# One maximum instruction for two heads, steps in the scores' ring, and loads one per chunk, in a two-layer attention kernel

## The chip, the core and the metric

The kernel runs on one core of a Trainium2 chip. The metric is the device time of one execution in microseconds, the median of several runs. The engines are TensorE (PE in the profile, its weight loads PEld), VectorE (DVE), ScalarE (ACT), GpSimd (POOL) and SyncE (SP), which here issues nearly all DMAs.

## What is computed

Two transformer layers over x (4 batches, 512 rows, 320 columns), all in float32, with a context of 1601 rows of 192 for each batch. A layer is self-attention, cross-attention over the context and a gated feed-forward, each with its own norm and residual:

```python
h1 = _ln(x, n1_g, n1_b)
x = _attn(h1, h1, q1, k1, v1, o1_w, o1_b, heads) + x
h2 = _ln(x, n2_g, n2_b)
x = _attn(h2, context, q2, k2, v2, o2_w, o2_b, heads) + x
h3 = _ln(x, n3_g, n3_b)
a, g = jnp.split(h3 @ ff_w1 + ff_b1, 2, axis=-1)
ff = a * jax.nn.gelu(g, approximate=False) @ ff_w2 + ff_b2
return ff + x
```

`_attn` is the usual softmax attention with 20 heads of 16 columns. The feed-forward's inner width is 1280.

## The kernel before

**Units.** The work is a list of units in order. In each layer there are 20 self-attention units (4 batches by 5 groups of 4 heads), 20 cross-attention units and 4 feed-forward units. The four heads of a group lie in four slots of 32 partitions, so that matmuls with 32 rows of contraction can run in the four row groups of TensorE side by side.

**Chunks and maxima.** An attention unit goes over its keys in chunks of 128: 4 chunks for self, 13 for cross. In `main` a chunk has two halves. Each half computes the transposed scores of two heads (`score`, tile st, line 1004), followed by the exponentials on ScalarE (line 1010, tile pr). Beside them it runs two matmuls for the *next* unit: those of `full_one` (tile sps, line 844) make the scores again with queries on the partitions, and VectorE takes their row maxima (line 852). The maxima, negated, become an extra row of the next unit's queries (`max_reduce`, `max_end`; DMAs q<-turned), so that the exponentials need no further subtraction. The rest of 65 keys in the cross-attention is done by `rest_two` (lines 858 and 868). After the two halves come the value products of the chunk before (`values`, tile av, line 1024, copied to vo by ScalarE and added to o by GpSimd at line 1041), then steps, then possibly extra rounds of four maxima, when `give` finds that the next units are owed more than the halves can hold.

**Steps.** Everything else is a step in one of several chains: queries (line 648, evacuated at 660), keys (674, 686), keys of the context (704, 714), values (779, 786 and 797, 806), projection of the attention's output (952, added to x at 959), norms and their transposes (461, 468), and the context's transposes (545). `steps` picks the one that is due first while a credit lasts; a round counter (two rounds to a chunk) stands for time. [...]

**Banks.** The eight PSUM banks are two rings of four: ps_st for scores and value products, ps_m for the maxima's scores and, in the main loop, the steps (`step_bank`). `quarter_banks` takes two of each in turn. In the feed-forward (`ff_main`) the values part of the gate is in ps_st and the gate part in ps_m. The last attention unit before a feed-forward has no maxima to make and spreads its four scores over both rings.

**Loads.** Inputs are loaded through SP's queue. `loads` is a queue of functions; one is run in each unit, after the maxima of the next unit have been finished (`c == u.nch - 3`). One such function issues all DMAs of a stage: `load_cross` 19, `load_self` 15, `load_out` 3. `load_first` (the feed-forward's first weights) is issued at once before the last cross-attention unit. The two functions rows_of_ones (line 132 and 135, GpSimd) are entries of this queue too. In layer 0 `add_context` turns the context by blocks and saves it to DRAM with one DMA; in layer 1 it is loaded back with one DMA and a wait of 8 rounds.

Of the kernel before, what the change touches and what calls it, by code (L numbers as in the profile page):

```python
# [19 lines left out]
FF = 4 * D  # L20
# [45 lines left out]
def kernel(ctx: ExitStack, tc: tile.TileContext, x, context, ws, out):  # L66
# [29 lines left out]
    ps_m = ctx.enter_context(tc.tile_pool(name="ps_m", bufs=4, space=PSUM))  # L96
# [53 lines left out]
    def load_x(b):  # L150
        src = x[b].rearrange("(c p) d -> p c d", p=P)
        for t in range(NQ) if b == 0 else (slice(NQ),):
            dma(out=xs[b][:, t], in_=src[:, t])
        loaded[b] = clock["round"]
# [23 lines left out]

    def load_rows(t, w, chunks):
        for k, at, n in chunks:  # L180
            dma(out=t[:n, k, :], in_=w[at : at + n, :])
# [22 lines left out]
    def load_self(l):  # L204
        load_norm(l, 0)
        load_rows(wq1, ws[l]["q1"], DK)
        load_rows(wk1, ws[l]["k1"], DK)
        load_rows(wv1, ws[l]["v1"], DK)

    def load_out(l, name):  # L210
        load_rows(wo, ws[l][name], DK)

    def load_cross(l):
        load_norm(l, 1)
        load_rows(wq2, ws[l]["q2"], DK)
        load_rows(wv2, ws[l]["v2"], CK)
        for t, n in ((wk_q, "k2"), (wv_q, "v2")):
            for i in range(4):
                dma(out=t[i * 32 : (i + 1) * 32], in_=ws[l][n].rearrange("(k p) d -> p k d", p=32))

    def load_ff(l):
        def small():
            load_norm(l, 2)
            with nc.allow_non_contiguous_dma(reason="a vector's elements go to partitions"):
                dma(out=b1, in_=ws[l]["ff_b1"].rearrange("(c p) -> p c", p=P))
            for half in range(2):
                dma(
                    out=w1r[half * REST : (half + 1) * REST, :],
                    in_=ws[l]["ff_w1"][2 * P :, half * FF : (half + 1) * FF],
                )  # L230

        loads.append(small)
        second = ws[l]["ff_w2"].rearrange("(c p) f -> p c f", p=P)
        for c in (slice(0, NHC // 2), slice(NHC // 2, NHC)):
            loads.append(lambda c=c: dma(out=w2[:, c], in_=second[:, c]))


    def load_first(l):

        load_rows(w1, ws[l]["ff_w1"], FK)  # L240
# [57 lines left out]

    chains = {n: deque() for n in ("divide", "project", "slots", "norm", "context", "early", "proj", "values")}
# [6 lines left out]

    start = {"on": True, "both": False, "quad": False}

    def step_bank(shape, name):

        if start["on"] and not start["both"]:
            return ps_st.tile(shape, F32, tag="st", name=name)
        return ps_m.tile(shape, F32, tag="m", name=name)
# [206 lines left out]
    def add_context(l, b, put, due, free):  # L520
        s = {}

        def tiles():
            s["cT"] = one.tile([P, KB, QT + 32], F32, tag="ctxT", name="ctxT")
            s["tail"] = one.tile([CK[0][2], 2, TAIL], F32, tag="tail", name="tail")

        def load():
            tiles()
            dma(out=s["cT"], in_=saved[b])
            dma(out=s["tail"], in_=saved_tail[b])  # L530
            s["round"] = clock["round"]

        if l:
            add("context", 0.0, load, due - 14, free)
            add("context", 0.0, lambda: put(s), due - 2, yes, lambda: clock["round"] >= s["round"] + 8)
            return

        def turn(i):
            if i == 0:
                tiles()  # L540
            c0, n = CGRP[i]
            t, _ = ctx_in.pop((b, i))
            for c in range(n):
                at = (c0 + c) * 32
                nc.vector.transpose(s["cT"][:, :, at : at + 32], t[:, c, :])
            if i + 2 < len(CGRP):
                load_context(b, i + 2)
            if i + 1 == len(CGRP):
                dma(out=saved[b], in_=s["cT"])
                s["last"] = t  # L550

        def tail():
            ps = step_bank([P, 2, P], "cps")
            for k, at, w in CK:
                nc.tensor.transpose(ps[:w, k, :TAIL], s["last"][:TAIL, 0, at : at + w], ident[:TAIL, :TAIL])
            w = CK[0][2]
            nc.scalar.copy(s["tail"], ps[:w, :, :TAIL])
            dma(out=saved_tail[b], in_=s["tail"])
            put(s)

        for i in range(len(CGRP)):
            add(
                "context", LIGHT, lambda i=i: turn(i), due - 2 * (len(CGRP) - i), free if i == 0 else yes,
                lambda i=i: clock["round"] >= ctx_in[b, i][1] + 4,
            )
        add("context", 0.3, tail, due)

# [30 lines left out]
    def add_proj(u):  # L598
# [97 lines left out]
        def keys_of_context():  # L696

            pss = quarter_banks("kps")
# [13 lines left out]
            for a, ps in enumerate(pss):  # L712
                copy = nc.vector.tensor_copy if a % 2 else nc.scalar.copy
                copy(stage[:, a, :], ps[:, : HALF + 32])
# [43 lines left out]
    def quarter_banks(name):  # L758

        return [  # L760
            pool.tile([P, 512], F32, tag=tag, name=name) for pool, tag in ((ps_st, "st"), (ps_m, "m")) * 2
        ]

    def add_values(u):
# [24 lines left out]
        def values_of_context(i, s):  # L789
# [3 lines left out]
            pss = quarter_banks("vps")  # L793
# [10 lines left out]
            for a, ps in enumerate(pss):  # L804
                copy = nc.vector.tensor_copy if a % 2 else nc.scalar.copy
                copy(vals[:, 4 * s + a, h0:h1, 0:DH], ps[:, :w].rearrange("p (h d) -> p h d", d=DH))
# [22 lines left out]
    def max_pairs(u):  # L829
# [7 lines left out]
        def max_bank(j):  # L837
            if start["both"] and j % 2 or start["quad"] and j == 1:
                return ps_st.tile([P, 512], F32, tag="st", name="sps")
            return ps_m.tile([P, 512], F32, tag="m", name="sps")  # L840

        def full_one(t, s, j):
            ps = max_bank(j)
            nc.tensor.matmul(  # L844
                ps,
                lhsT=u.q[j * SLOT : (j + 1) * SLOT, t * P : (t + 1) * P],
                rhs=u.kT[j * SLOT : (j + 1) * SLOT, u.k0 + s * 512 : u.k0 + (s + 1) * 512],
                start=True,
                stop=True,
            )  # L850
            to = u.nm[:, j * NQ + t : j * NQ + t + 1] if ns == 1 else u.pm[:, t, j, s : s + 1]
            return lambda: nc.vector.tensor_reduce(to, ps, AX.X, ALU.max, negate=(ns == 1))  # L852

        def rest_two(heads):
            pss = [max_bank(j) for j in heads]
# [10 lines left out]
            def reduce():  # L866
                for j, ps in zip(heads, pss):
                    nc.vector.tensor_reduce(
                        u.pm[:, :, j, full],
                        ps[:, : NQ * rest].rearrange("p (t w) -> p t w", w=rest),  # L870
# [7 lines left out]
            deque(  # L878
                [lambda t=t, s=s, j=j: full_one(t, s, j) for j in heads] for s in range(full) for t in range(NQ)
            )  # L880
# [115 lines left out]
    def main(u, give, nxt):  # L996
# [3 lines left out]
        def score(c, j, pool=ps_st, tag="st"):  # L1000
            r = min(P, u.nkeys - c * P)
            rows = slice(j * SLOT, (j + 1) * SLOT)
            st = pool.tile([P, N], F32, tag=tag, name="st")
# [41 lines left out]
        for c in range(u.nch):  # L1045
            extra = []
            if last:

                round_of(
                    [  # L1050
                        lambda j=j, ring=ring: score(c, j, *ring)
                        for j, ring in zip(range(HG), ((ps_st, "st"), (ps_m, "m")) * 2)
                    ],
                    [],
                )
# [13 lines left out]
            start["quad"] = True  # L1069
# [4 lines left out]
            start["quad"] = False  # L1074
            if not last and c == u.nch - 3:
                max_reduce(nxt)
                max_end(nxt)
                if loads:
                    loads.popleft()()
# [21 lines left out]
    def ff_main(u, give, nxt):  # L1101
# [20 lines left out]
        rings = ((ps_st, "st"), (ps_m, "m"))  # L1122

        def full(c, i):
            ps = rings[i][0].tile([P, 512], F32, tag=rings[i][1], name="fps")
# [22 lines left out]
        for c in range(0, NHC, 2):  # L1148

            beside(True, 2)  # L1150
            pss = [[full(c, 0), full(c, 1)]]
            beside(False, 2)
            pss.append([full(c + 1, 0), full(c + 1, 1)])
# [24 lines left out]
    def before(u):  # L1178
# [6 lines left out]
        if u.kind == "cross" and u.m == B * G - 1:  # L1185
            load_first(u.l)
# [4 lines left out]
    def after(u):  # L1191

        stage[u.b] += 1
        if u.b == B - 1:
            load_bias(u.l, ("self", "cross", "ff").index(u.kind) + 2)
            if u.kind == "self":
                loads.append(lambda: load_out(u.l, "o2_w"))
            if u.kind == "cross" and u.l + 1 < L:
                loads.append(lambda: load_out(u.l + 1, "o1_w"))
            if u.l + 1 < L:  # L1200
                if u.kind == "ff":
                    for k in kbuf[1:]:
                        rows_of_ones(k, False)
                    loads.append(lambda: load_cross(u.l + 1))
                    load_ff(u.l + 1)
                elif u.kind == "self":
                    loads.append(lambda: load_self(u.l + 1))
# [63 lines left out]
    load_x(0)  # L1271
    load_self(0)
# [22 lines left out]
    load_x(1)  # L1295
    rows_of_ones(kbuf[0][:, 4 * QT :])
    for k in kbuf[1:]:
        loads.append(lambda k=k: rows_of_ones(k))
    loads.insert(0, lambda: load_x(2))
    loads.append(lambda: load_out(0, "o1_w"))  # L1300
    loads.append(lambda: load_x(3))
    loads.append(lambda: load_cross(0))
    load_ff(0)
# [7 lines left out]
    for i, u in enumerate(units):  # L1311
        nxt = units[i + 1] if i + 1 < len(units) else None
        before(u)
        if u.kind == "ff":

            flush()
            until(lambda: u.hT is not None, "norm")
# [36 lines left out]
```

## Time and profile before

| | us |
|---|---|
| median of 3 runs (3267.23 to 3268.77) | 3267.34 |
| the profiled execution's own time | 3268.32 |
| its span, first to last instruction | 3266.6 |
| PE busy | 3209.3 (98%) |
| DVE busy | 2170.3 (66%) |
| ACT busy | 1973.4 (60%) |
| POOL busy | 1219.4 (37%) |

The self-attention of layer 0 lasts to about 350 us of the span, its cross-attention to about 1375, its feed-forward to about 1675; layer 1 follows in the same order. A row of a group gives the line, the engine, the operation, what it writes and reads, how many there are, and busy time and mean; the arrow `<-` in brackets names what ended the idle time before an instruction. Busy time of PE is a union of overlapping matmuls, four of which often run at once; the granted clock was 0.996 on average.

### The profile page before, as it was taken

The numbers are of one execution on the slowest core, as the hardware profiler recorded it, in microseconds if no ns is written. First come the engines' busy times: TensorE is split into PE (matmuls) and PEld (weight loads), VectorE is DVE, ScalarE is ACT, GpSimd is POOL, SyncE is SP. The second block draws the span as 40 slices with busy tenths as digits, with TensorE's granted clock in tenths as the row PEclk, the third lists the DMA queues.
The fourth block names the chain that finished last, engine by engine and source line by source line (L and its number), as shares of the span: only waits on it lengthen the run. The fifth ranks groups of instructions, "written<-read, shape, count | busy, mean of one in ns | idle before, by whom it ended". The sixth has DMA issues, their size and how long they took to land.

```text
span 3266.6 us, 83246 instructions
## 1 busy us (share of the span) xinstructions
PE 3209.3 (98%) x33970; PEld 1495.2 (46%) x33970; DVE 2170.3 (66%) x4076; ACT 1973.4 (60%) x3951; POOL 1219.4 (37%) x1627
## 2 busy tenths in 40 slices
PE   8899999999999999999999999999999999999999
PEld 4344444444444444355444444444444444443555
DVE  7677777777877777523247777877777787784221
ACT  4666567677777777711136665677778777775110
POOL 5545334344434434211235553344344434332000
PEclk9999999999999999999999999999999999999999
DMA  1211001100100100100003000010010010001000
GB/s 47 54 47 32 16 20 26 51 16 15 42 17 17 38 13 11 40 1 1 1 9 70 26 12 17 13 37 16 16 27 14 16 30 11 16 10 37 9 10 14
DMA packets 91281, 74.54 MB, mean 23 GB/s; under 512 B 41612, under 2 KB 83988, under 8 KB 89364
## 3 DMA queue, kind: packets, MB, share of 16 engines
q1 hardware_dynamic: 90816, 69.22, 8.7%
q8 instruction: 268, 4.39, 0.6%
q14 instruction: 113, 0.93, 0.1%
q0 software_dynamic: 64, 0.00, 0.0%
q10 hardware_dynamic: 20, 0.00, 0.0%
HBM read 33.04 MB, written 7.93 MB: 13 GB/s over the span
## 4 chain that ended last, share of the span: by engine, by line
PE 61%; DVE 4%; POOL 1%; DMA 0%; issue 0%; ACT 0%; SPq 0%; DVEq 0%; POOLq 0%
PE st L1004 14%; PE av L1024 12%; PE fps L1127 9%; PE sps L844 9%; PE yps L1162 5%; PE fps L1139 2%; PE ops L952 2%; PE kps L704 2%; PE qps L648 2%; PE vps L797 2%; DVE pm L852 1%; DVE nmax L852 1%; PE sps L858 1%; PE hps L461 1%; PE kps L674 1%; PE vps L779 1%
## 5 line engine op out<-in xcount | busy, mean ns | idle before, releaser
L1010 ACT ACTIVATE pr<-st 128x512 f32<-128x512 f32 (+1 forms) x2720 | 1414.0, 601 | 498.5 <-PE sps L844 370.8
L1004 PE MATMUL st<-q,kT 32*128 32x512 f32 (+1 forms) x5440 | 1377.7, 615 | 19.0 <-DVE nmax L852 6.3
L852 DVE TENSOR_REDUCE pm<-sps 128x1 f32<-128x512 f32 x1920 | 1191.7, 681 | 241.2 <-PE sps L844 237.3
L844 PE MATMUL sps<-kT,q 32*128 32x512 f32 x5120 | 1326.2, 621 | 11.5 <-DVE pm L852 6.3
L1041 POOL TENSOR_TENSOR o<-o,vo 128x512 f32<-128x512 f32 x576 | 734.0, 1274 | 1412.3 <-ACT vo L1040 1224.4
L1004 PEld LDWEIGHTS st<-q,kT 32*128 32x128 f32 (+1 forms) x5440 | 511.4, 181 | 509.8 <-ACT pr L1010 295.1
L1024 PE MATMUL av<-pr,vals 128*32 128x512 f32 (+1 forms) x5440 | 729.8, 605 | 2.0 <-ACT pr L1010 2.0
L844 PEld LDWEIGHTS sps<-kT,q 32*128 32x128 f32 x5120 | 453.9, 184 | 146.8 <-issue 73.7
L852 DVE TENSOR_REDUCE nmax<-sps 128x1 f32<-128x512 f32 x640 | 395.6, 680 | 134.6 <-PE sps L844 133.4
L1040 ACT COPY vo<-av 128x512 f32<-128x512 f32 x576 | 347.0, 602 | 46.0 <-PE av L1024 42.5
L1024 PEld LDWEIGHTS av<-pr,vals 128*32 128x32 f32 (+1 forms) x5440 | 109.9, 108 | 497.7 <-ACT pr L1010 479.3
L1127 PE MATMUL fps<-hT,w 128*128 128x512 f32 x640 | 288.0, 599 | 0.0
L1145 ACT ACTIVATE gl<-fps,b 128x512 f32<-128x512 f32 x80 | 54.8, 687 | 376.6 <-PE fps L1139 376.6
L596 POOL TENSOR_SCALAR q<-qst,keep,zero 64x128 f32<-64x128 f32 (+1 forms) x476 | 231.8, 487 | 50.0 <-ACT qst L660 16.1
L1127 PEld LDWEIGHTS fps<-hT,w 128*128 128x128 f32 x640 | 117.4, 190 | 147.1 <-issue 140.9
L1146 DVE SCALAR_TENSOR_TENSOR hid<-fps,b,gl 128x512 f32<-128x512 f32 x48 | 35.8, 750 | 153.0 <-ACT gl L1145 150.6
L952 PE MATMUL ops<-wo,aT 112*32 112x160 f32 (+1 forms) x3072 | 127.4, 302 | 9.0 <-DMA aT<-o 9.0
L952 PEld LDWEIGHTS ops<-wo,aT 112*32 112x32 f32 (+1 forms) x3072 | 99.4, 111 | 77.0 <-issue 52.4
L648 PE MATMUL qps<-hT,wq 112*32 112x128 f32 (+3 forms) x2880 | 125.9, 309 | 3.5 <-DVE nmax L852 2.5
L648 PEld LDWEIGHTS qps<-hT,wq 112*32 112x32 f32 (+1 forms) x2880 | 84.7, 110 | 87.4 <-issue 47.1
L474 POOL TENSOR_TENSOR x<-x,brow 128x320 f32<-128x320 f32 x96 | 83.6, 889 | 90.5 <-DVE hn L448 79.3
L409 POOL TENSOR_SCALAR root<-root 128x4 f32<-128x4 f32 x23 | 5.3, 231 | 297.3 <-DVE root L403 296.7
(88 smaller groups left out, 2233.4 us busy)
## 6 DMA issues: line engine op xcount, KB each, us to landing
kT<-kst SPq DMA_DIRECT2D x320, 48.0 KB
aT<-o SPq DMA_DIRECT2D x320, 32.0 KB
q<-turned SPq DMA_DIRECT2D x636, 1.0 KB
ctxT<-ctxT SPq DMA_DIRECT2D x8, 1248.0 KB
w<-in_L_xattn_ff_w_dram SPq DMA_DIRECT2D x4, 1280.0 KB
ctxin<-in_ctx_dram SPq DMA_DIRECT2D x24, 192.0 KB
w<-in_L_xattn_ff_w_dram SPq DMA_DIRECT2D x4, 800.0 KB
kT<-kst SPq DMA_DIRECT2D x160, 8.0 KB
```

The source lines that it names most:

```text
L596: nc.gpsimd.tensor_scalar(to, stage[rows, :w], keep[b][rows], more[rows], ALU.mult, ALU.add)
L648: nc.tensor.matmul(ps[to, :w], lhsT=wq[:n, k, gs], rhs=first.hT[:n, k, at[i] : at[i] + w], start=(k == 0), stop=(k == 2),)
L844: nc.tensor.matmul(ps, lhsT=u.q[j * SLOT : (j + 1) * SLOT, t * P : (t + 1) * P], rhs=u.kT[j * SLOT : (j + 1) * SLOT, u.k0 + s * 512 : u.k0 ...
L852: return lambda: nc.vector.tensor_reduce(to, ps, AX.X, ALU.max, negate=(ns == 1))
L952: nc.tensor.matmul(ps[f : f + m, : D // 2], lhsT=aT[:n, k, t * P + f : t * P + f + m], rhs=wo[:n, k, cols], start=(k == 0), stop=(k == 2),)
L1004: nc.tensor.matmul(st[:r, :], lhsT=u.kT[rows, u.k0 + u.cols[c] : u.k0 + u.cols[c] + r], rhs=u.q[rows, :], start=True, stop=True)
L1010: nc.scalar.activation(p[:r], st[:r], AF.Exp)
L1024: nc.tensor.matmul(ps[i * SLOT : (i + 1) * SLOT, :], lhsT=columns_of[:r, head : head + SLOT], rhs=pr.pop((c, j))[:r, :], start=True, stop= ...
L1040: nc.scalar.copy(vo, ps)
L1041: nc.gpsimd.tensor_tensor(u.o, u.o, vo, ALU.add)
L1127: nc.tensor.matmul(ps, lhsT=w1[:, k, i * FF + c * P : i * FF + (c + 1) * P], rhs=u.hT[:, k, :], start=(k == 0), stop=False,)
L1162: nc.tensor.matmul(ps[:, :D], lhsT=hid[c][:, t * P : (t + 1) * P], rhs=w2[:, c, :], start=(c == 0), stop=(c == NHC - 1),)
```

## The change

Three things change together.

1. ps_m becomes two tiles of two banks. The two heads of a half write the two banks of one tile, and one maximum instruction reads both (`full_two`, `rest_two`). In extra rounds, and in the feed-forward, the first two heads use two banks of ps_st instead and are reduced singly.
2. Steps take their bank from ps_st. `quarter_banks`, the last unit's scores and the gates of the feed-forward are rearranged to fit: two single banks of ps_st and one pair.
3. The entries of `loads` become single transfers, one is run at the end of *every* chunk, and what is left is issued before a feed-forward. Large loads are cut: x 1 to 4, the feed-forward's w1 2 to 10 and w2 2 to 10. The save of the turned context is cut in six, its load in three, with waits of 2 rounds between them and 4 after the last.

The core of the diff:

```diff
-    ps_m = ctx.enter_context(tc.tile_pool(name="ps_m", bufs=4, space=PSUM))
+    ps_m = ctx.enter_context(tc.tile_pool(name="ps_m", bufs=2, space=PSUM))
...
-        if start["on"] and not start["both"]:
-            return ps_st.tile(shape, F32, tag="st", name=name)
-        return ps_m.tile(shape, F32, tag="m", name=name)
+        if start["on"] and start["both"]:
+            return ps_m.tile([P, 2, 512], F32, tag="m", name=name)[:, 0]
+        return ps_st.tile(shape, F32, tag="st", name=name)
...
-            return lambda: nc.vector.tensor_reduce(to, ps, AX.X, ALU.max, negate=(ns == 1))
...
+        def banks(heads):
+            if start["both"] and heads[0] == 0:
+                pss = [ps_st.tile([P, 512], F32, tag="st", name="sps") for _ in heads]
+                return pss, [ps.rearrange("p (o w) -> p o w", o=1) for ps in pss]
+            ps = ps_m.tile([P, 2, 512], F32, tag="m", name="sps")
+            return [ps[:, i] for i in range(2)], [ps]
+
+        def full_two(heads, t, s):
+            pss, parts = banks(heads)
...
+            def reduce():
+                n = 2 // len(parts)
+                for i, part in enumerate(parts):
+                    j = heads[0] + i
+                    nc.vector.tensor_reduce(to[:, j : j + n], part, AX.X, ALU.max, negate=(ns == 1))
...
+        both = ps_m.tile([P, 2, 512], F32, tag="m", name=name)
+        singles = [ps_st.tile([P, 512], F32, tag="st", name=name) for _ in range(2)]
+        return [singles[0], both[:, 0], singles[1], both[:, 1]], singles, both
...
-            start["quad"] = True
+            start["both"] = True
             for i, e in enumerate(extra):
...
-            start["quad"] = False
+            start["both"] = False
             if not last and c == u.nch - 3:
                 max_reduce(nxt)
                 max_end(nxt)
-                if loads:
-                    loads.popleft()()
+            if loads:
+                loads.popleft()()
...
-            add("context", 0.0, load, due - 14, free)
-            add("context", 0.0, lambda: put(s), due - 2, yes, lambda: clock["round"] >= s["round"] + 8)
+            for k in range(0, KB, 2):
+                add("context", 0.0, lambda k=k: load(k), due - 14 + k, free if k == 0 else yes, later(2) if k else yes)
+            add("context", 0.0, lambda: put(s), due - 2, yes, later(4))
...
-            load_first(u.l)
+            loads.extend(load_first(u.l))
...
-                    loads.append(lambda: load_cross(u.l + 1))
-                    load_ff(u.l + 1)
+                    loads.extend(load_cross(u.l + 1))
+                    loads.extend(load_ff(u.l + 1))
                 elif u.kind == "self":
-                    loads.append(lambda: load_self(u.l + 1))
+                    loads.extend(load_self(u.l + 1))
...
+            now(loads)
+            loads.clear()
```

## The prediction

> **What bounds the kernel now.** I read the page's busy shares first, then the costliest groups, then the timeline of one ordinary stretch of the cross-attention, then the waits of the maxima, and last the two stretches where the windows view showed TensorE idle.
>
> ```profile
> PE 3209.3 (98%) x33970; PEld 1495.2 (46%) x33970; DVE 2170.3 (66%) x4076; ACT 1973.4 (60%) x3951; POOL 1219.4 (37%) x1627
> ```
>
> TensorE is busy all the time and is the bound; a gain must be a stretch in which it waits, or streams fewer matmuls than it could. The change removes no matmul. The ordinary chunk:
>
> ```profile
> 705.42 0.70 PE L1004 MATMUL st<-q,kT 32*128 32x512 f32 x2
> 705.43 0.70 PE L844 MATMUL sps<-kT,q 32*128 32x512 f32 x2
> 705.58 0.62 ACT L1040 COPY vo<-av 128x512 f32<-128x512 f32 x1
> ...
> 706.58 2.06 ACT L1010 ACTIVATE pr<-st 128x512 f32<-128x512 f32 x4 [0.38 <-PE sps L844]
> 706.66 2.48 DVE L852 TENSOR_REDUCE pm<-sps 128x1 f32<-128x512 f32 x4 [0.44 <-PE sps L844]
> ...
> 707.35 1.07 PE L1024 MATMUL av<-pr,vals 128*32 128x512 f32 x8
> 708.23 0.84 PE L648 MATMUL qps<-hT,wq 112*32 112x128 f32 x24
> ...
> 709.00 0.70 PE L1004 MATMUL st<-q,kT 32*128 32x512 f32 x2
> ```
>
> The reader should see the slack. Counted from 705.42, four maxima end at 3.72 us; the next chunk starts at 3.58 here because a step (qps) lies between, and at 2.93 without one (702.49 to 705.42 is such a chunk). A ring of one chunk's maxima therefore has little to spare, and whatever else VectorE is given (the division, a norm) makes TensorE wait for a bank. Who pays is in the view of line 852:
>
> ```profile
>   PEld sps L844: 28.0, 51
>   PEld st L1004: 26.8, 19
>   PEld qps L648: 25.8, 41
>   POOL o L1041: 19.8, 4
>   PEld hps L461: 14.5, 17
>   PE st L1004: 11.1, 18
> ```
>
> (us, times.) The view goes on with vps 14.0 us in 22 waits, sps as matmul 6.3 in 1, cps 4.0 in 4 and ops 3.6 in 12. The last kind of loss is the DMA queue:
>
> ```profile
> 150.46 1.88 SPq L219 DMA_DIRECT2D w<-in_L_xattn_k_dram  x4
> 152.38 1.89 SPq L219 DMA_DIRECT2D w<-in_L_xattn_v_dram  x4
> 154.38 3.51 SPq L943 DMA_DIRECT2D aT<-o  x4
> ...
> 162.90 1.56 PE L952 MATMUL ops<-wo,aT 96*32 96x160 f32 x20 [8.96 <-DMA aT<-o]
> ```
>
> ```profile
> 589.20 0.64 DVE L545 STREAM_TRANSPOSE ctxT<-ctxin 128x192 f32<-128x192 f32 x2 [7.28 <-DMA ctxin<-in_ctx_dram]
> ```
>
> ```profile
> 153.30:162.90 9.60, 0.64 (x21) 0.33 (x14) 1.55 (x4) 1.04 (x2) 0.00 (x0) 0.65 0.94 175
> 162.90:166.60 3.70, 3.70 (x56) 2.91 (x56) 0.65 (x2) 0.00 (x0) 0.00 (x0) 0.52 0.00 0
> 584.60:591.40 6.80, 0.56 (x4) 0.00 (x0) 2.06 (x7) 1.24 (x3) 0.00 (x0) 0.88 0.54 152
> 591.40:597.10 5.70, 5.64 (x20) 2.71 (x20) 5.33 (x11) 1.19 (x2) 0.00 (x0) 0.55 0.01 3
> ```
>
> (Columns: PE, PEld, DVE, ACT, POOL busy, granted clock, DMA share, GB/s.) Twice TensorE stands still behind a bundle of weight loads issued at once, and afterwards works at half its clock.
>
> **The change part by part.**
>
> *Loads one per chunk.* The bundle of load_cross(0) is 19 DMAs in one go, 144.25 to 154.27 us, six vectors of 0.4 KB and about 2.6 MB of weights; aT<-o is issued after it and its projection waits 9.1 us (the pack before it came at 153.62, the usual distance is 0.14). Then 3.7 us at clock 0.52 lose 3.7 x 0.48 = 1.8. The second bundle (load_self(1), 15 DMAs from 577.0 to 585.2) delays the context rows; a DVE transpose waits for them, the maxima queue behind it on VectorE, TensorE loses 6.4 us, and 5.7 x 0.45 = 2.6 at the low clock. Sum: 10.9 + 9.0 = **-20**. With one load per chunk at most some four stand between two SP waits: the largest, 240 KB, at about 215 GB/s (rate while the bundle moved) is 1.1 us, so four in a row hold a small transfer for 4.5 us at worst, and the queue of SP runs ahead of TensorE by more than that. I keep +1 for it. Bounds: -22, and -9 if one stall stays. Added DMAs: x 9, w2 16, w1 16, the saved context 20 in stores and 8 in loads = 69; at 0.45 us of SP's time each (three issues in 1.36 us in SP's timeline) that is 31 us on a queue that mostly waits: 0. The context's load in layer 1 is now in thirds, the last issued 4 rounds (about 6.6 us, half a chunk each) before it counts as there; the whole 1248 KB took 5.2 us at 2656.06, so a third takes about 2: 0.
>
> [...] The rows say that the pieces have time to spare. [...] by the rows it is 0, since TensorE stood still for over 3 us twice in 3.3 ms, both times behind a bundle. [...]
>
> *One maximum instruction for two heads.* Four in a row take 2.48 us: 0.68 for one and 0.60 spacing. From 260 elements in 0.42 us (line 868) and 512 in 0.68, one element costs 1.03 ns, so 1024 take about 1.21 us and, back to back, 0.60 + 0.53 = 1.13. Two take 2.34 instead of 2.48: VectorE ends 0.14 us earlier per chunk, 0.07 per pair, 1280 pairs, 90 us less DVE busy time. [...] I take 0.07. What counts is only where TensorE waits for a maximum's bank: 28.0 + 26.8 + 11.1 + 6.3 = 72 us in 89 waits. A weight load waits first while the previous pass, 0.43 us, still streams, so about 72 - 89 x 0.43 = 34 us is loss. Each wait ends 0.14 us earlier, 0.28 after an extra round of four maxima: **-14** (bounds -5, where another step of the chain is late next, namely the exponentials, and -34).
>
> *Steps in the scores' ring.* Steps waited for a maximum's bank in qps 25.8, hps 14.5, vps 14.0, cps 4.0, ops 3.6 = 62 us, 96 waits; less 96 x 0.43 = 21 us lost. A step now takes the bank of the chunk's second score, whose exponential ends at 706.58 + 1.03 = 707.6, before the step at 708.23: **-18**, and 3 left where ScalarE is late. The added wait: the next chunk's scores need the step's evacuation (line 959, 660, 686, 786). Before, maxima needed it: 23 us in 64 waits for line 959. With a step the fourth score comes two packs later (0.96 us) and needs what the last maximum needed, so the cost moves and does not grow: 0 (bounds -3 and +80, see the rivals). If it waits, an exponential is queued behind it on ScalarE and the next value product behind that.
>
> *The rest.* The two rows_of_ones (1.49 + 3.74 us on POOL at 67.46) now fall in neighbouring chunks of unit 1 rather than in two units: the sum o<-o,vo is late, the pr buffers are held, ScalarE and then TensorE wait. Once each now costs about 1; I take +3 (0 to +8). At the start and in the feed-forward the gate pairs, extra maxima and steps share rings two deep: +3 (0 to +6). The quarter banks of context keys and values, and the last units' scores in a pair, hold as many banks as before: 0.
>
> Sum: -20 + 1 - 14 - 18 + 3 + 3 = **-45**. Against the profiled execution's own time of 3268.3 us (span 3266.6 and 1.7 around it) this is 3223; the median of the runs is 1.0 us lower, so about 3223 to 3222. Since several of these waits end on TensorE together, I take off a fifth of the two ring terms (6 us): **3229**. About 0.2% (6.5 us) is what a measurement of this kernel can tell from no change.
>
> **Rivals.**
>
> 1. *Only the DMA stalls go* (chance 0.24). Where a maximum's bank was late an exponential is late next; for it speaks that st waits for ACT pr in 446 places (295.1 us of weight-load idle). Then -20 + 1 - 5 + 6 = -18: 3249.
> 2. *More comes free* (0.13). A late bank tears a pack of four into singles (at 1686 to 1691 sps come one or two at a time)[...]. If the pairs mend them, the 34 + 21 us double, less what was counted: about -85: 3182.
> 3. *Slower: steps starve ScalarE* (0.1). Place: every chunk with a step, some 530 of them by the code (120 queries, 80 keys, 128 values, 128 projections, 72 transposes, 4 tails). A score that waits for the step's evacuation holds all following exponentials, and ScalarE has 2.7 of the chunk's 2.93 us taken (2.06 + 0.62). If each step costs 0.15 us more, +80 - 19 - 14 - 18 + 6 = +35: 3302. It decides from about 0.08 us per step (45 / 530). Against it: the evacuations are short (0.28 to 0.38 us) and end before the fourth score in the chunk shown.
> 4. *Nothing measurable* (0.05): the stalls come back at another small transfer, and ring gains are eaten by late exponentials: within 3261 to 3274.
>
> **How the numbers follow.** The forecast (0.48) is 3229, its own range 3208 to 3245 from the bounds above. Faster by over 0.2%: 0.48 + 0.24 + 0.13 = 0.85; within: 0.05; slower: 0.1. Leaving out rival 3 (0.1) and the far part of rival 2 gives 3190 to 3264.
>
> **What would show it.** Right: no gap over 3 us before ops at about 160 and at 590, clock 0.9 or better there; L852 in half as many instructions of about 1.2 us; DVE busy near 2080; qps and hps no longer waiting for pm or nmax. Wrong: st waiting for L959 or L660 by more than 60 us in total (rival 3); a maximum of 1024 elements over 1.36 us; a new wait for aT, q<-turned or ctxT.

## The result, and the profile after

The change brings the median to 3248.84 us, from 3268.06 us beside it: 19.2 us less, a ratio of 0.994 with a 95% interval of 0.9923 to 0.9957. The forecast was 3229, some 39 us less, and half of that came. The time lies in the whole range of 3190 to 3264, but outside the forecast's own, 3208 to 3245. The profiled execution has a span of 3248.2 us, 18.4 less than before.

First the page of the kernel after, busy shares and the group of the maxima (busy us, mean ns, idle before it and what ended it):

```profile
PE 3197.9 (98%) x33970; PEld 1481.1 (46%) x33970; DVE 2061.2 (63%) x2663; ACT 1969.5 (61%) x3951; POOL 1217.6 (37%) x1627
...
L896 DVE TENSOR_REDUCE pm<-sps 128x2 f32<-128x1024 f32 (+1 forms) x970 | 1136.1, 1206 | 273.1 <-PE sps L880 265.5
```

VectorE has 109 us less to do (2061 for "near 2080"), of which 72 are these maxima's (1587.3 us before, 1514.9 now), and one merged maximum takes 1.21 us. TensorE's work is the same, and only 11 of its busy microseconds are gone. The two stalls behind the bundled loads are away; the windows view of the kernel after, at the places that answer to 162.9 and 591.4 us of before (same columns as there):

```profile
160.00:165.50 5.50, 5.50 (x102) 3.22 (x96) 4.15 (x9) 2.53 (x6) 1.38 (x2) 1.00 0.01 3
589.00:593.00 4.00, 4.00 (x54) 1.70 (x42) 2.34 (x3) 3.19 (x7) 1.61 (x2) 1.00 0.35 92
```

TensorE is busy throughout, at full clock. Now who waits for a maximum (line 896, the successor of line 852):

```profile
  POOL o L1088: 70.6, 10
  PEld st L1051: 42.4, 43
  PE st L1051: 18.8, 21
  PEld sps L880: 6.9, 16
  PE sps L880: 2.0, 4
  PEld vps L807: 1.1, 2
```

The steps (qps, hps, vps, cps, ops: 62 us before) are gone from the list but for 1.1. The waits of the scores, though, stand at 42.4 + 18.8 + 6.9 + 2.0 = 70 us, where they were 72. Read as the prediction read this view, the maxima gained nothing. That reading turns out to be wrong.

Two things are new in the trace. One is an early gap. The timeline of the kernel after, 71 to 82.5 us:

```profile
71.32 3.57 POOL L135 TENSOR_SCALAR kT<-kT,zero,ones 64x1664 f32<-64x1664 f32 x2
...
76.60 3.54 POOL L135 TENSOR_SCALAR kT<-kT,zero,ones 64x1664 f32<-64x1664 f32 x2
80.22 1.26 POOL L1088 TENSOR_TENSOR o<-o,vo 128x512 f32<-128x512 f32 x1
81.51 0.60 ACT L1057 ACTIVATE pr<-st 128x512 f32<-128x512 f32 x1 [9.31 <-POOL o L1088]
...
82.16 1.22 PE L1051 MATMUL st<-q,kT 32*128 32x512 f32 x1 [7.10 <-ACT pr L1057]
```

The two rows_of_ones run one behind the other on GpSimd; the sum o+vo comes after both, ScalarE's exponential waits 9.31 us for it, and TensorE 7.10. The other is a wait of VectorE's merged copy of the context's values (line 834), 48 times; what it sat idle for, in the kernel after:

```profile
  ACT vals L833: 86.4, 48
```

and one of these places in the timeline of the kernel after:

```profile
2125.37 0.56 DVE L834 COPY vals<-vps 128x384 f32<-128x384 f32 x1 [2.13 <-ACT vals L833]
...
2125.85 2.54 DVE L896 TENSOR_REDUCE pm<-sps 128x2 f32<-128x1024 f32 x2
2125.98 0.30 PEld L880 LDWEIGHTS sps<-kT,q 32*128 32x128 f32 x4 [0.30 <-DVE vals L834]
```

The copy stands on VectorE until ScalarE has written its two slots, two maxima queue behind it, and the next pack of maxima's scores waits for the bank. Chunks with such a step take 0.45 us more than before (mean) in 38 places of the cross-attention and 0.34 in 8 more: 38 x 0.45 + 8 x 0.34, some 20 us by the trace.

**Theories.** Mine: the rings did bring the expected gain, and two side effects that the sum had at 0 and at +3 took it back. The rival is the prediction's own first one, whose 3249 is the measured time: the rings bring nothing, because wherever a maximum was late an exponential is late next.

### The profile page after: what moved, and what is told of

It is laid out like the page before. It is cut to its first block, busy times and chain, and to the rows that moved or that the text cites. A ratio compares the mean times of both kernels' runs of the same rounds, so it can differ in the third digit from the quotient of the medians.

```text
span 3248.2 us, 81861 instructions
## 1 busy us (share of the span) xinstructions
PE 3197.9 (98%) x33970; PEld 1481.1 (46%) x33970; DVE 2061.2 (63%) x2663; ACT 1969.5 (61%) x3951; POOL 1217.6 (37%) x1627
## 4 chain that ended last, share of the span: by engine, by line
PE 93%; DVE 2%; POOL 2%; issue 1%; ACT 1%; DMA 0%; SPq 0%; POOLq 0%; DVEq 0%
PE st L1051 25%; PE av L1071 20%; PE sps L880 14%; PE fps L1167 9%; PE yps L1206 5%; PE ops L998 3%; PE kps L732 3%; PE qps L676 3%; PE vps L825 3%; PE fps L1179 2%; PE vps L807 2%; PE sps L904 1%; PE kps L702 1%; PE hps L478 1%; DVE pm L896 1%
## 5 line engine op out<-in xcount | busy, mean ns | idle before, releaser
L896 DVE TENSOR_REDUCE pm<-sps 128x2 f32<-128x1024 f32 (+1 forms) x970 | 1136.1, 1206 | 273.1 <-PE sps L880 265.5
L880 PE MATMUL sps<-kT,q 32*128 32x512 f32 x5120 | 1285.0, 623 | 2.3 <-DVE nmax L896 2.0
L896 DVE TENSOR_REDUCE nmax<-sps 128x2 f32<-128x1024 f32 (+1 forms) x343 | 378.8, 1145 | 156.7 <-PE sps L880 153.5
L880 PEld LDWEIGHTS sps<-kT,q 32*128 32x128 f32 x5120 | 408.6, 184 | 108.4 <-issue 87.0
L676 PEld LDWEIGHTS qps<-hT,wq 112*32 112x32 f32 (+1 forms) x2880 | 86.4, 110 | 79.2 <-issue 36.2
```

The source lines that it names most:

```text
L676: nc.tensor.matmul(ps[to, :w], lhsT=wq[:n, k, gs], rhs=first.hT[:n, k, at[i] : at[i] + w], start=(k == 0), stop=(k == 2),)
L880: nc.tensor.matmul(ps, lhsT=u.q[j * SLOT : (j + 1) * SLOT, t * P : (t + 1) * P], rhs=u.kT[j * SLOT : (j + 1) * SLOT, u.k0 + s * 512 : u.k0 ...
L896: nc.vector.tensor_reduce(to[:, j : j + n], part, AX.X, ALU.max, negate=(ns == 1))
```

## The experiments

All times are medians; each kernel ran beside the kernel before on the same chip, and the difference is to that.

| kernel | us | before beside it | difference | ratio, 95% interval |
|---|---|---|---|---|
| after | 3248.84 | 3268.06 | -19.2 | 0.9940 (0.9923 to 0.9957) |
| e1_loads | 3251.99 | 3268.03 | -16.0 | 0.9949 (0.9936 to 0.9963) |
| e2_rings | 3263.35 | 3268.03 | -4.7 | 0.9987 (0.9981 to 0.9994) |
| e3_vals | 3232.21 | 3268.03 | -35.8 | 0.9887 (0.9874 to 0.9901) |
| e4_rows | 3235.86 | 3268.03 | -32.2 | 0.9903 (0.9890 to 0.9917) |
| e5_both | 3224.99 | 3268.61 | -43.6 | 0.9861 (0.9846 to 0.9876) |
| e6_split | 3258.86 | 3268.61 | -9.8 | 0.9967 (0.9955 to 0.9980) |
| e7_steps | 3270.86 | 3268.61 | +2.3 | 1.0010 (1.0002 to 1.0018) |
| e8_vo | 3272.45 | 3268.61 | +3.8 | 1.0012 (1.0005 to 1.0018) |
| e9_divide | 3296.43 | 3269.04 | +27.4 | 1.0085 (1.0071 to 1.0099) |
| e11_steps_m | 3251.55 | 3269.04 | -17.5 | 0.9949 (0.9936 to 0.9961) |
| e12_later | 3199.30 | 3267.80 | -68.5 | 0.9789 (0.9776 to 0.9802) |
| e13_spread | 3200.61 | 3267.80 | -67.2 | 0.9795 (0.9781 to 0.9808) |

### The two halves of the change

e1_loads is the kernel before with the loads part alone (every line of the diff that concerns `load_...`, `loads`, and the saved context), e2_rings the kernel before with all the rest.

> The kernel before with the loads part of the change alone: single transfers, one per chunk, context stored and loaded in pieces; rings, maxima and steps as before. Theory (the stalls behind the two bundles are 20 us, and the two rows_of_ones, which fall in neighbouring chunks with this part, cost about 6 of it): 3253 to 3256, that is 12 to 15 us below before, no gap over 3 us before ops near 160 us or near 590 us, a gap of some 7 us near 82 us. Rival (the stalls were only half the DMA queue's, the low clock or the next transfer gives them back): under 8 us below before. Rival 2 (rows_of_ones cost what the prediction said, 3): 3249 to 3251.

> The kernel before with the rings part of the change alone: pairs of heads in one tile, one maximum instruction for both, steps in the scores' ring, pairs in the quarter banks; loads bundled as before. Theory (the rings' 30 us came, and some 20 us were lost where VectorE's merged copy of the context's values waits for ScalarE's copy): 3258 to 3264, 4 to 10 us below before, with the wait of the vals copy on VectorE for ScalarE over 70 us in total. Rival (prediction's rival 1: an exponential is late wherever a maximum's bank was, the rings give at most 5): 3268 to 3285, no faster than before or slower.

The halves add up: -16.0 and -4.7 make -20.7, for -19.2 of both. e1_loads is 1 us faster than its theory's 3253 to 3256; e2_rings is inside its 3258 to 3264, and the copy's wait stands at 86.3 us in it. The loads part is as the sum had it: chunk by chunk against before, the two stalls give -10.9 and -8.8 and the rows_of_ones cost +6.2 and -0.9 in two successive chunks. So that half works and pays nearly all that the whole change paid. The loads of the two bundles keep their sizes in it and are only spread over the chunks; what the cutting of the other loads does alone was not measured. The rings' half has a gain and a loss inside it, or nothing.

### The merged copy's wait

e3_vals is the kernel after with the four slots dealt out differently: ScalarE writes the first two, VectorE the last two.

```diff
-            pss, singles, both = quarter_banks("vps")
+            _, singles, both = quarter_banks("vps")
+            pss = singles + [both[:, 0], both[:, 1]]
 ...
-                nc.scalar.copy(vals[:, 4 * s + 2 * a, h0:h1, 0:DH], ...)
+                nc.scalar.copy(vals[:, 4 * s + a, h0:h1, 0:DH], ...)
 ...
-                vals[:, 4 * s + 1 : 4 * s + 4 : 2, h0:h1, 0:DH],
+                vals[:, 4 * s + 2 : 4 * s + 4, h0:h1, 0:DH],
```

> The kernel after with one thing changed: in the copy of the context's values ScalarE writes slots 4s and 4s+1 and VectorE's merged copy writes 4s+2 and 4s+3, instead of even and odd slots in turn. Same instructions, sizes and engines; only VectorE's strided write no longer spans ScalarE's. Theory: the wait for ScalarE's copies goes (86.4 us of VectorE's idle time in 48 places), the 46 steps with values of the context take 0.4 us less each, 3228 to 3232, 17 to 20 us below after. Rival (the chunks with these steps are late for another reason, four copies on ScalarE and VectorE that are read later, or an exponential that is late next): the wait goes, the time stays within 4 us of after, 3245 to 3250.

-35.8 against -19.2: 17 us back, just short of what the theory expected. What the copy (line 835 in e3_vals) sits idle for is now TensorE:

```profile
  PE vps L826: 66.5, 48
```

The same instructions, sizes and engines cost 17 us or nothing, by where they write. In the kernel after, VectorE's single write with a stride of two slots reaches across a slot that ScalarE writes, and it waits for that copy (86.4 us in 48 places); no data of the one is in the other. But such a stride does not always bring the wait. The merged copy of the context's keys (line 742) is dealt out to the two engines in the same way, and in the kernel after it waits for TensorE alone:

```profile
  PE kps L732: 62.8, 40
```

Why the values' copy waits and the keys' does not stays open.

### The rows of ones

```diff
-        loads.append(lambda k=k: rows_of_ones(k))
+        rows_of_ones(k)
```

> The kernel after with the two rows_of_ones (of the key buffers of later units) run at the start, where GpSimd is idle, instead of in two neighbouring chunks of unit 1. Theory: the gap of 7.5 us near 82 us goes, 6 to 8 us below after: 3241 to 3243. The prediction's value was 3 us: 3246. Rival (the gap covers a transfer or a weight that is late anyway, so another wait takes its place): within 1.5 us of after.

-32.2 against -19.2: 13 us back, more than any of the expectations. The trace gives 9.0 of it at the place expected (that chunk goes from 14.5 to 5.5 us, below the 7.7 of before, since before paid for one of the two there). Most of the rest is no effect of the edit. It is the clock, in the windows view of the same stretch of the two profiled executions, first of after, then of e4_rows:

```profile
1761.00:1764.00 3.00, 2.52 (x11) 1.80 (x14) 1.50 (x5) 2.04 (x5) 0.00 (x0) 0.56 0.00 0
```

```profile
1750.00:1753.00 3.00, 2.61 (x22) 1.21 (x22) 2.45 (x6) 2.65 (x7) 0.00 (x0) 1.00 0.00 0
```

In both, TensorE had just waited 1.23 us for an exponential. After it the granted clock is 0.56 in the one and 1.00 in the other, and 11 matmuls run in 3 us instead of 22. This chunk and those at 148, 1848 and 1856 us make 4.3 us between the two profiles. e3_vals, which did not touch the rows of ones, is rid of the same 4.3, and loses 2.6 in chunks at 53 and 1052 us where the clock did not fall in after. So the edit's own share is 9 us; where the clock falls is not the same in these kernels (in e5_both it falls in the chunks at 134 and 225 us and at none of those four). Added up over a profile, the clock record stands at 0.5 for 27.3 us in after, 21.1 in e3_vals, 10.2 in e4_rows and 20.8 in e5_both; about half of such time is lost, an estimate from the 11 matmuls for 22 above.

### Both repairs, and what the merging is worth

e5_both has both repairs. e6_split is e5_both with two single maxima on each pair's tile:

```diff
-                n = 2 // len(parts)
-                for i, part in enumerate(parts):
+                for i, ps in enumerate(pss):
                     j = heads[0] + i
-                    nc.vector.tensor_reduce(to[:, j : j + n], part, AX.X, ALU.max, negate=(ns == 1))
+                    nc.vector.tensor_reduce(to[:, j : j + 1], ps, AX.X, ALU.max, negate=(ns == 1))
```

> The kernel after with both repairs: ScalarE writes the context values' slots 4s and 4s+1 and VectorE the next two, and both rows_of_ones run at the start. Theory (the two losses are separate): what each gave alone adds up, -17 and -9 to -13, so 3219 to 3224. Rival (both free the same time, since either leaves ScalarE as the next to be late): 3228 to 3233, no better than the first repair alone.

> The version with both repairs, but each tile of two banks gets two maxima of one head, 128x512 each, instead of one of 128x1024; tiles, rings and steps as there. It isolates the merging. By the prediction's term for the merging (0.07 us per pair, only where TensorE waits for a bank): 10 to 15 us above the version with both repairs. Rival (what counted was that pairs share one tile, or the steps' ring; VectorE's 90 us are off the path): within 3 us of it. Rival 2 (a bank of a pair comes free only after both maxima, so the split costs the fixed time at every late chunk twice): 15 to 40 us above.

e5_both takes 3224.99, one microsecond above the interval expected: 24.4 us below after, where the repairs one by one gave 16.6 and 13.0. In the profiled executions it is 23.8 for 20.1 and 14.5, and the time at half clock explains, by that estimate, some 8 of the difference of 10.8. e6_split is 33.9 us slower than e5_both. So the merged instruction alone, on the same tiles, is worth 34 us: two and a half times the prediction's 14, its upper bound, and far from the rival ("the rings give at most 5"). It lies within the 15 to 40 of the second rival for e6_split, but mostly for another reason.

How 97 us less VectorE time at places that hardly show in the waits give 34 us is seen in one chunk after a division. The timeline of e6_split:

```profile
870.22 1.26 POOL L1088 TENSOR_TENSOR o<-o,vo 128x512 f32<-128x512 f32 x1 [7.09 <-ACT vo L1087]
870.33 1.45 DVE L974 TENSOR_TENSOR oturn<-oturn,rd 128x256 f32<-128x256 f32 x1
...
872.44 4.37 DVE L896 TENSOR_REDUCE pm<-sps 128x1 f32<-128x512 f32 x7
872.51 0.30 PEld L1051 LDWEIGHTS st<-q,kT 32*128 32x128 f32 x4 [0.84 <-ACT pr L1057]
872.51 1.13 PE L1051 MATMUL st<-q,kT 32*128 32x512 f32 x4
...
873.75 0.30 PEld L881 LDWEIGHTS sps<-kT,q 32*128 32x128 f32 x4 [0.94 <-DVE pm L896]
873.75 1.13 PE L881 MATMUL sps<-kT,q 32*128 32x512 f32 x4
```

and the same chunk in e5_both:

```profile
861.07 0.41 DVE L975 TENSOR_TENSOR oturn<-oturn,rd 128x256 f32<-128x256 f32 x1
...
861.22 1.39 POOL L1089 TENSOR_TENSOR o<-o,vo 128x512 f32<-128x512 f32 x1 [7.07 <-ACT vo L1088]
...
862.15 4.78 DVE L897 TENSOR_REDUCE pm<-sps 128x2 f32<-128x1024 f32 x4
...
863.29 0.70 PE L1052 MATMUL st<-q,kT 32*128 32x512 f32 x2
...
863.39 0.70 PE L881 MATMUL sps<-kT,q 32*128 32x512 f32 x2
```

In e5_both two heads' scores and two of the maxima's run as one pack of four, 0.1 us apart. In e6_split the maxima are late, so the scores run alone for 1.13 us, and then the maxima's scores run alone for 1.13 us. A wait of 0.94 us is listed, but these eight matmuls take 2.37 us (872.51 to 874.88), where e5_both runs the first eight in 1.22 (863.29 to 864.51), and the chunk takes 4.48 us instead of 3.28.

The maxima are late because of the division's multiplication on VectorE (oturn by rd), which stands before them in the queue: 1.45 us in e6_split, 0.41 in e5_both. It is a race with GpSimd's sum o+vo. In e6_split the sum began 0.1 us before the multiplication, which ended only 0.28 us after the sum; in e5_both the multiplication began first. So it goes throughout before, after, e5_both and e6_split: all 90 multiplications that began after such a sum and beside it took 0.74 to 1.45 us, and each ended 0.28 us after the sum; all 158 that began first, and had such a sum start beside them, took 0.41 to 0.43. With the merged maxima VectorE arrives sooner, mostly in time: in this chunk 0.15 us before the sum in e5_both, 0.11 after it in e6_split. The group of the multiplication, in e6_split and in e5_both:

```profile
L974 DVE TENSOR_TENSOR oturn<-oturn,rd 128x256 f32<-128x256 f32 x80 | 63.8, 797 | 0.1
```

```profile
L975 DVE TENSOR_TENSOR oturn<-oturn,rd 128x256 f32<-128x256 f32 x80 | 41.2, 514 | 0.1
```

At 26 places it is long in e6_split and short in e5_both. These chunks and the ones after them differ by 23.1 us of the 34.9 between the two traces; some 3 more are the clock's (27.3 us at half clock for 20.8). At 26 places too, all but one of them the same, before is 24.6 us slower than after. So most of what the merging gives is this race won. That is read from the traces; no run here changes the race alone.

### The steps alone

```diff
-        if start["on"] and not start["both"]:
-            return ps_st.tile(shape, F32, tag="st", name=name)
-        return ps_m.tile(shape, F32, tag="m", name=name)
+        if start["on"] and start["both"]:
+            return ps_m.tile(shape, F32, tag="m", name=name)
+        return ps_st.tile(shape, F32, tag="st", name=name)
```

> The kernel before with one thing changed: steps take a bank of the scores' ring instead of the maxima's, outside the stretch at the start; four single banks for maxima, single maximum instructions, bundled loads. By the prediction's term for the steps: 18 us below before, 3250. By the prediction's rival 3 (steps starve ScalarE): above before. Theory from the chunks of the kernels seen so far (most chunks with queries, values or projections gain 0.0 to 0.2 us): 8 to 15 us below before, 3253 to 3260.

All of these were wrong: +2.3, a ratio of 1.0002 to 1.0018. The waits of the steps for a maximum are gone as in the kernel after, and the view of qps in e7_steps shows what stands in their place (before: 21.7 and 7.1 us for nmax and pm):

```profile
  issue: 34.9, 114
  ACT pr L1010: 29.0, 97
```

28.8 us of waiting for VectorE have become 29.0 of waiting for ScalarE. With hps, vps, cps and ops taken in, 87 us of waits for exponentials have come for the 62. Here the rival's reason holds: the step waits for the exponential that would have been late next anyway. The profiled execution took 3274.54 us, with 44.4 us at half clock for 28.1 before; without that it would be an estimated 1 to 2 us faster than before (half of such time lost, as above), which is next to nothing too.

e11_steps_m asks the reverse, e5_both with the steps in the pairs' ring:

```diff
-        return ps_st.tile(shape, F32, tag="st", name=name)
+        if start["on"] or name == "cps":
+            return ps_st.tile(shape, F32, tag="st", name=name)
+        return ps_m.tile([P, 2, 512], F32, tag="m", name=name)[:, 0]
```

> The version with both repairs, with the steps (outside the start, and but for the tails of the context) in a pair's tile of the maxima's ring instead of a bank of the scores' ring. Theory (steps alone were worth nothing with four single banks, but with two pairs a step takes half of the ring and tears the packs of the chunks it stands in): 20 to 80 us above the version with both repairs, so the move of the steps is what lets the pairs pay. Rival (the ring of the steps is indifferent with pairs too): within 5 us.

It loses 26 us to e5_both (-17.5 against -43.6), as expected. With four single banks the steps' ring is indifferent; with two pairs a step holds half of the ring. The move of the steps gains nothing by itself, but without it the pairs would cost 26 us.

### Which engine is late: moving work to VectorE and away from it

e8_vo is e5_both with every third copy of vo on VectorE, e9_divide is e5_both with the division's multiplication on GpSimd:

```diff
-                nc.scalar.copy(vo, ps)
+                (nc.vector.tensor_copy if c % 3 == 1 else nc.scalar.copy)(vo, ps)
```

```diff
-            nc.vector.tensor_tensor(
+            nc.gpsimd.tensor_tensor(
                 turned[:, :, :DH], turned[:, :, :DH],
```

> The version with both repairs, with the copy of the value product's second half (vo) on VectorE instead of ScalarE in every third chunk. It moves about 0.6 us per three chunks from ScalarE to VectorE. If ScalarE's exponentials are what is late next (rival 1's reason), it is 5 to 25 us below the version with both repairs; if VectorE's maxima still are, 5 to 30 us above, since VectorE's copy delays a maximum by 0.6 us; within 3 us if neither is.

> The version with both repairs, with the 80 multiplications of the division (oturn by rd, 128x256, 41.2 us of VectorE in that version) on GpSimd. The mirror of moving vo to VectorE. Theory (where VectorE is the last to be ready, each us of it costs 0.35 to 0.42 us of the whole, as the two shifts of 97 and 111 us gave): 14 to 17 us below the version with both repairs; 5 to 14 if the chunks with a division are not among the late ones any more. Rival (GpSimd's sum o+vo, 1.28 us each and waited for by ScalarE, queues behind the multiplication): 0 to 15 us above.

e8_vo is 47 us slower than e5_both, beyond what I had expected for that side: 111 us more on VectorE cost far more than 79 less on ScalarE bring. The mirror failed. e9_divide is 71 us slower than e5_both. The view of the transpose after the multiplication (line 979) tells why:

```profile
  POOL oturn L975: 152.6, 78
```

The transpose is the next thing in VectorE's queue, so VectorE stands 1.95 us each time until GpSimd is through with o+vo and the multiplication, with the maxima behind it. I had counted the work that leaves VectorE and not the wait that comes.

e12_later issues that transpose as a step of its own two rounds later; e13_spread does so too, with the multiplication on VectorE again:

```diff
         def divide():
             nc.vector.tensor_tensor(
 ...
+            when.append(clock["round"])
+
+        def back():
             nc.vector.transpose(u.o, turned.rearrange("p b s -> p (b s)"))
 ...
+        add("divide", LIGHT, back, r - 20, yes, since(2, 2))
-        add("divide", 0.0, turn, r - 20, lambda: u.g or held["open"] < 2, since(2, 1))
+        add("divide", 0.0, turn, r - 20, lambda: u.g or held["open"] < 2, since(3, 1))
```

> As the version with the multiplication on GpSimd, but VectorE's transpose after it is issued two rounds (one chunk) later as a step of its own, so that VectorE need not stand and wait for GpSimd. If the loss of +71 us there was VectorE waiting for GpSimd (152.6 us of idle time ahead of the transpose) with the maxima queued behind: the wait goes, and the 41 us taken from VectorE give 5 to 17 us below the version with both repairs, 3208 to 3220. If GpSimd's own queue was the cause: still 20 us or more above it.

> The version with both repairs, with the division's transpose two rounds (one chunk) later than its multiplication, both on VectorE as before. No work is taken from VectorE, it is only spread. If single chunks are late because 0.95 to 1.2 us of extra work fall into one (3.28 and 4.18 us instead of 2.93): 5 to 12 us below the version with both repairs. If the sum of VectorE's work over several chunks counts: within 3 us. What the previous kernel gains over this one is then due to GpSimd doing the multiplication.

Both are about 24 us faster than e5_both and the fastest of all: 3199.3 and 3200.6, or 68 us below before. They differ by the multiplication's engine alone, so with the transpose moved nothing is left of the loss of e9_divide: it was the wait. But the two equal each other although VectorE has 36 us less to do in e12_later (2020.9 against 2056.4): VectorE's sum no longer counts here. And the gain of e13_spread is larger than either answer, since the edit did more than I meant. Between the same value products of e5_both and e13_spread, some 11 of its 27.5 us of span are gained up to the first chunks of the first cross-attention, some 6 in the second self-attention, and 11 in all the rest. The clock alone makes an estimated 8 of the 27.5 (4.6 us at half clock for 20.8, half of it lost). The added step shifts the other steps of the self-attention. Who waits there for GpSimd's o+vo, first in e5_both, then in e13_spread:

```profile
  ACT pr L1058: 26.4, 31
```

```profile
  ACT pr L1062: 11.7, 20
```

In e5_both thirteen small operations of a norm's root stand before o+vo at 133 us; ScalarE waits 2.88 us, TensorE 1.23, and the clock falls (0.79 over that stretch). In e13_spread the root begins after o+vo. So a good part of this gain is a lucky order on GpSimd's queue; what spreading the division alone is worth was not measured apart.

## Why the prediction was right, and where it was not

- **DMA stalls, -20 (+1).** Right: -19.7 by the two chunks of e1_loads. The prediction took its 69 more DMAs at 0; with them this half gave -16.0, and neither place of the stalls shows a wait for a piece. The loads behind the two stalls were not made smaller.
- **Merged maximum, -14.** The saving on VectorE was right, its price was not: -34, where steps and pairs are given. The duration was well read (1.21 us, two in 2.36 for 2.34). e6_split against e5_both shows 77.8 us less for the maxima of line 896 with 1247 instructions fewer, 62 ns, near the 70 taken. What failed is "Each wait ends 0.14 us earlier", a price in proportion to the wait. It took the division as a fixed load on VectorE, whereas its multiplication takes 0.41 or up to 1.45 us by whether it starts before GpSimd's sum, and 23 of the 34 us lie there. The prediction's rival 2 had the torn packs that follow from it, as a chance, but not their cause.
- **Steps in the scores' ring, -18.** Failed: +2 alone. The 62 us of waits vanished from the view and came back as 87 us of waits for exponentials. The bound that "another step of the chain is late next" was put beside the merging, where it did not bite, and not here, where it did. The danger of rival 3 (3302) did not come either.
- **Quarter banks, 0.** Failed: +17, by e3_vals. The sum counted banks and durations of the merged copy, and not what it has to wait for: ScalarE's copy of a slot that lies between the two it writes.
- **rows_of_ones, +3 (0 to +8).** Mis-sized: +5 by the trace of e1_loads; taking both away gives 9.
- **Start and feed-forward, +3.** About right: the feed-forward's chunk takes 3.8 us more (312.25 against 308.43), the start 1 to 2.
- **Pairs on a ring of two.** Not in the sum. By difference, e6_split is 13 to 17 us slower than the loads, the steps and the rows' repair make it (-16.0, +2.3, and -9 to -13 against its -9.8). That includes the feed-forward's 3.8; the rest, a pair's two banks coming free together, was only argued.

So 3249, rival 1's number, came out with another cause. By the runs it is -16 (loads) +2 (steps) +13 to +17 (pairs) -34 (merging) +17 (the copy's wait), in sum -14 to -18 for -19.2 measured. Since the pairs were taken by difference, this sum proves nothing about them; that it lands on rival 1's number is luck. With the two side effects repaired the change gives -43.6, close to the sum of -45, but partly because two wrong terms, -14 and -18, make as much as -34 does. Faster, at a chance of 0.85, came true.

## What to carry to other kernels

A sum over waits in the profile is no price: before it is trusted, ask of each wait what ends next (if that is just as late, the wait is worth nothing, as with the steps, +2.3 us alone), and whether some instruction's duration depends on when it starts (then a little time is worth more than it shows, as with the multiplication beside GpSimd's sum, 0.41 or up to 1.45 us): look for a group whose mean lies well above its shortest. When two instructions are merged, list what the new one reads and writes and which other engine's work lies between; dealing out whole blocks of the values to each engine cost nothing here, dealing out every second one 17 us (and nothing for the keys, so the trace has to be asked). When an operation is moved to an idle engine, look at where its reader stands in its own queue: in e9_divide VectorE's queue stood 1.95 us at each of 78 transposes, and with the transpose moved later too (e12_later) the time went from 27.4 us above before to 68.5 below.

## What was not expected of the hardware

- A pause of TensorE of 1.23 us was followed by a granted clock of 0.56 in one kernel and 1.00 in another, at the same instructions. What decides between the two is not shown by any run here. Four chunks in which the clock fell in after make 4.3 us between the two profiles, so a chunk that gains 1 to 2 us between two profiles proves little.
- The same multiplication on VectorE took 0.41 us when it began before GpSimd's sum, and up to 1.45 us when it began after it, in 90 of 90 cases.
- Two merged maxima of 1024 elements take 2.36 us, four of 512 2.48: the merging saves little time on VectorE, and two thirds of the 34 us come from the race that it wins.
